# Three gathers ahead of a weighing, a shorter first run of side steps, and a norm tile on GpSimd

## The chip, the cores and the metric

The kernel runs on one core of a Trainium2 chip. A core has five engines with instruction queues of their own: TensorE (PE, matrix products and transposes into PSUM; its weight loads are listed as PEld), VectorE (DVE), ScalarE (ACT), GpSimd (POOL) and SyncE (SP, which here issues nearly all DMAs). Each engine takes its instructions strictly in the order in which the program wrote them, and waits for the others through semaphores. The metric is the device time of one execution in microseconds; lower is better.

## The reference

The model is four pairs of an attention and a feed-forward part on x of shape 8 x 512 x 128, all in float32, each part with a layer norm ahead of it and a residual addition behind it:

```python
x = x + _L0_attn_ref(_layernorm(x), ...)   # batch norm, sigmoids, attention without softmax
x = x + _L0_ffn_ref(_layernorm(x), ...)    # 16 experts on every 16-wide piece of a token, best 2
x = x + _L1_attn_ref(_layernorm(x), ...)   # linear attention
x = x + _L1_ffn_ref(_layernorm(x), ...)    # shared expert, and one of 8 for chosen tokens
x = x + _L2_attn_ref(_layernorm(x), ...)   # 16 heads, softmax over the queries
x = x + _L2_ffn_ref(_layernorm(x), ...)    # 8 low-rank experts, 2 given ones per token
x = x + _L3_attn_ref(_layernorm(x), ...)   # 21-tap convolution along the tokens
x = x + _L3_ffn_ref(_layernorm(x), ...)    # gated, weights and activations rounded to 4 bits
```

Two parts matter here. In layer 0's feed-forward every token is cut into 8 pieces of 16 numbers; a softmax over 16 experts is taken for each piece, the two best experts are kept with their weights, and their outputs are added:

```python
w = jax.nn.softmax(t @ expert_emb, axis=-1)
topw, topi = jax.lax.top_k(w, K)                       # K = 2 of 16
hmid = jax.nn.gelu(jnp.einsum('td,edi->tei', t, W1) + b1, approximate=False)
eo = jnp.einsum('tei,eio->teo', hmid, W2) + b2
comb = (jnp.take_along_axis(eo, topi[:, :, None], axis=1) * topw[:, :, None]).sum(axis=1)
```

In layer 2's feed-forward each token of the first 1024 has two given experts. Rows are ordered by expert, each expert is applied to its own rows, and the results go back to their tokens, weighted:

```python
order = jnp.argsort(flat_e, stable=True); bin_ids = flat_e[order]; tok = order // top_k
xr = x.reshape(T, hs)[tok]
for e in range(E):
    h = jax.nn.gelu(xr @ w1A[e].T @ w1B[e], approximate=False)
    out = out + (bin_ids == e)[:, None] * (h @ w2A[e].T @ w2B[e])
y = jnp.zeros((T, hs), xr.dtype).at[tok].add(flat_w[order][:, None] * out)
```

## The kernel before

x stays in SBUF as eight blocks (b = 0 to 7) of 512 tokens, each as four tiles (j) of 128 tokens by 128 features. The order of work on each engine is written out by hand: the program says in which order Python calls the pieces, and every engine's queue is the sequence of its instructions in that order.

**Layer 0, attention, second run.** After the batch norm, `run` walks a list of stages over the blocks; in iteration i each stage works on block i plus its lag, in the order of the list. For block b the residual is added (`attended`, L274), statistics are taken (`stats`: four bn_stats and bn_aggr on DVE, L732 and L734, then 1/sqrt on POOL, L246 and L247, and the scaled mean on POOL, L737). In the next iteration `scale` makes the four norm tiles `xn` (L743 on ACT, L349 on POOL). Its argument `own` says how many tiles ACT makes; the rest go to POOL. In the first run it is called with its default, three and one; in the second run with J = 4, all on ACT. `turned` transposes them on PE an iteration later, `hidden` and `logits` follow, `spikes` puts sigmoids on ACT and a product on POOL (L392), `biased` adds a bias on POOL (L352). The list also calls three steps of block 0's choice in each iteration once it is under way, and filler matmuls (`keep_clock`).

**Layer 0, experts.** There are 128 units (b, e), 16 experts for each block, worked through in pipeline order: at index n, the first product and the GELUs of unit n (`first_half`, L569 and L570 on ACT), then the second product of unit n - 2 on PE and its weighting on DVE (`second_half`, L582), then its addition on POOL (L588). The weights come from DRAM: `choice(b)` works out on DVE (and a little on POOL) which two experts each piece keeps, in twelve steps; the last transposes the result and writes it to the DRAM tensor `gates[b]` with four DMAs (L477). `spread` reads four experts' weights of a block, repeated over 16 partitions, into one of three buffers `gs` with eight DMAs (L550) on SP. `fetch` calls it for the k-th spread (block k // 4) once `gates` of that block has been written in program order and, from k = 3 on, not before 4 * (k - 2) units are done. The steps of the choices of blocks 1 to 7 and of some other preparations are side steps: `side` takes the next one. After the second half of each index one side step is taken, at indices 0 and 1 five each. Within an index, `fetch` comes before the side step.

**Layer 2, frames.** Layer 2's attention is 64 frames, one per pair of heads of a block. A frame n makes scores for two key tiles at a time (`scores(n, 0)` and `scores(n, 1)`: PE, the maximum on DVE, L1629, exponentials on ACT, L1635), scales the values by the sums (`weigh(n, 0)` and `weigh(n, 1)`: a reciprocal on DVE, L1649, a product on POOL, L1650), multiplies (`context(n)`, one frame later on PE), and projects queries, keys, values and output for the frames around it. Projections have two forms: `project(n)`, in half arrays in an interleaved order (L1556) with marks on SP (L1523) between, and the plain calls `queries`, `output`, `values` (L250). The plain form is taken in the frames listed in `moving`. Other work is hung into a frame at five hooks: P inside the first scores, V after them, G after the first weighing, D after the second scores, E after the second weighing. Steps are put there with `at(frame, hook, f)`.

**Expert rows.** Layer 2's feed-forward runs beside it for blocks 0 and 1, in class `Rows`. In frame 8b + 9 the eight sets of 128 normalised rows are scattered by POOL's indirect DMAs into ordered slots in DRAM; in frame 8b + 10 they are loaded, and `products` applies the experts to 15 slots, ending with `last(0)` and `last(1)`, which copy the results out of PSUM (L1894) and write them to `slots_out` (L1895). In frame 8b + 11, hook E, `back` gathers four of the eight sets of rows with indirect DMAs on POOL (L1933); in 8b + 12, hook G, the other four. `add` adds them to x on DVE, weighted (L1946), in frame 8b + 12, hook E, and 8b + 13, hook V.

Of the kernel before, what the change touches and what calls it, by code (L numbers as in the profile page):

```python
# [26 lines left out]
D = 128  # L27
NB = 8
TB = 512
J = TB // P  # L30
# [134 lines left out]
def body(ctx, tc, dram, spans, x_in, ib, it, ic, ei, out):  # L165
# [114 lines left out]
    def layer0():  # L280
# [7 lines left out]
        with ExitStack() as st:  # L288
# [54 lines left out]
            def scale(b, own=3):  # L343
                l0[b]["xn"] = xn = norm.tile([P, J, D], F32, tag="xn", name="xn")
                nb, rs = l0[b]["by"]
                scaled(xn, x[b], (nb, rs), own)
                for j in range(own, J):
                    r1, n1 = rs[:, j : j + 1], nb[:, j : j + 1]
                    nc.gpsimd.tensor_scalar(xn[:, j, :], x[b][:, j, :], r1, n1, ALU.mult, ALU.add)  # L349
# [139 lines left out]
            with (  # L489
                tc.tile_pool(name="a0h", bufs=1) as hp,  # L490
                tc.tile_pool(name="a0", bufs=2) as ap,
                psum({"one": 8}),
                tc.manual_schedule(),
            ):
                hs = [hp.tile([P, NB, TB], F32, tag=f"h{k}", name=f"h{k}") for k in range(3)]
                bst = [hp.tile([P, NB, 6], F32, tag=f"bst{k}", name=f"bst{k}") for k in range(3)]

                def run(stages, iterations):
                    for i in iterations:
                        for f, lag in stages:  # L500
                            if 0 <= i + lag < NB:
                                f(i + lag)

                run(
                    (
                        (scale, 2),
                        (stats, 3),
                        (turned, 1),
                        (project, 0),
                        (lambda b: biased(b, "bp"), -2),  # L510
                    ),
                    range(-3, NB + 2),
                )
                keep_clock(22)
                sc, bi = batch_norm()
                expand()
                run(
                    (
                        (turned, -2),
                        (lambda b: scale(b, J), -1),  # L520
                        (turn_v, 3),
                        (logits, -3),
                        (attended, 0),
                        (stats, 0),
                        (spikes, 4),
                        (gram, 2),
                        (gram_out, 1),
                        (hidden, -2),
                        (exponentials, -3),
                        (lambda b: chosen(3), -4),  # L530
                        (lambda b: biased(b, "bo"), -1),
                        (lambda b: keep_clock(6), -3 - NB // 2),
                    ),
                    range(-4, NB + 3),
                )
                chosen(20)
# [106 lines left out]
            with tc.manual_schedule():  # L643
# [36 lines left out]
                def second(n):  # L680

                    if n >= 2:
                        b, e = units[n - 2]
                        second_half(b, e, hms.pop(n - 2), gs[(n - 2) // 4][:, e % 4, :])
                        fetch(n - 1)
                    for _ in range(1 if n > 1 else 5):
                        side("V", n)

                for n in range(len(units) + 2):
# [716 lines left out]
    def late():  # L1406
# [11 lines left out]
        with tc.tile_pool(name="a2", bufs=2) as wp, tc.tile_pool(name="l3", bufs=1) as lp:  # L1418
# [5 lines left out]
            def at(frame, hook, *fs):  # L1424
                steps.setdefault((frame, hook), []).extend(fs)
# [273 lines left out]
            class Rows:  # L1699
# [116 lines left out]
                def products(self, meanwhile, ahead):  # L1816
# [63 lines left out]
                    def last(k, d):  # L1880
# [8 lines left out]
                                mm(two[g % 2][:, at_(i)], d[r, at_(i)], self.w2b(g))  # L1889
                        n = min(8, n_slots - 8 * k)  # L1890
                        dst = S[:, 8 * k : 8 * (k + 1), :].rearrange("p (i m) d -> p i m d", m=2)
                        for m, f in enumerate((nc.scalar.copy, nc.vector.tensor_copy)):
                            w_ = (n + 1 - m) // 2
                            f(dst[:, :w_, m, :], two[m][:, : w_ * P].rearrange("p (i d) -> p i d", d=D))  # L1894
                        nc.sync.dma_start(  # L1895
# [27 lines left out]
                    last(0, d0)  # L1923
                    last(1, d1)

                def back(self, js):
                    if js[0] == 0:
                        self.rows = both("cg").rearrange("p (n d) -> p n d", d=D)
                    for j in js:
                        for k in range(2):  # L1930
                            n = 2 * j + k
                            at_ = 8 * self.b + n
                            nc.gpsimd.indirect_dma_start(  # L1933
                                self.rows[:, n, :],
                                None,
                                slots_out[self.b],
                                bass.IndirectOffsetOnAxis(spots[:, at_ : at_ + 1], 0),
                            )

                def add(self, js):  # L1940
                    xb = x[self.b]
# [374 lines left out]
            for b in range(2):  # L2316
# [7 lines left out]
                at(8 * b + 9, "G", lambda r_=r_: r_.put((4,)))  # L2324
                at(8 * b + 9, "E", lambda r_=r_: r_.put((5, 6, 7)))
                at(8 * b + 10, "V", r_.load)
                at(8 * b + 11, "E", lambda r_=r_: r_.back((0, 1)))
                at(8 * b + 12, "G", lambda r_=r_: r_.back((2, 3)))
                at(8 * b + 12, "E", lambda r_=r_: r_.add((0, 1)))
                at(8 * b + 13, "V", lambda r_=r_: r_.add((2, 3)))  # L2330
            for b in range(NB - 1):
# [252 lines left out]
            with tc.manual_schedule():  # L2584
# [12 lines left out]
                            steps.pop((n, "S"), ()),  # L2597
                        )

                moving = {8 * b + k for b in range(2) for k in (9, 12)}  # L2600
                for n in range(N):
                    first_scores(n)
                    hook(n, "V")
# [74 lines left out]
```

## Time and profile before

| what | value |
|---|---|
| time, median of 3 runs | 1398.86 us (1398.42 to 1400.73) |
| profiled execution, its own time | 1393.95 us |
| its span, first to last instruction | 1392.2 us |
| PE busy | 1327.5 us, 95% |
| DVE busy | 1014.3 us, 73% |
| ACT busy | 1014.6 us, 73% |
| POOL busy | 642.4 us, 46% |
| DMA queue of SP and ACT | 28.3% of 16 engines' span |

The profile lists start times in microseconds from the first instruction. A line of a timeline names start, duration, engine, source line, operation, tile written and tiles read, and how often; in brackets stands the idle time before it and who ended it. The chain of waits is followed back from the last instruction: at each step to what released it or to the instruction before it on its engine, so what is on it is what set the end. SPq is SP's queue issuing a DMA; how long a DMA takes from there to landing is listed with the line that issues it. Matmuls are pipelined, so a busy PE is not one at its peak. In the frames, PE's granted clock is full; in one stretch of 3.4 us near 107 us it is half.

### The profile page before, as it was taken

The page shows a single profiled execution, that of the slowest core. Times are in us where ns is not written, and L with a number is a line of the kernel's source. Part 1 is how long each engine was busy: PE and PEld are TensorE (multiplying, and loading weights), DVE is VectorE, ACT ScalarE, POOL GpSimd, SP SyncE. Part 2 cuts the span into 40 slices and gives each one's busy share as a digit, 9 for nine tenths or more (in the row PEclk, how much of TensorE's full clock was granted, in tenths as well). Part 3 has the DMA queues.
Part 4 walks back from the last instruction along what each step waited for, and adds up shares of the span by engine and source line. Part 5 has one row for each costly group of instructions (what it writes and reads, how often), then busy time and mean ns, then how long its engine had stood idle before and what let it go on. Part 6 is the DMA issues. An engine that isn't in the chain of part 4 may idle for free.

```text
span 1392.2 us, 33106 instructions
## 1 busy us (share of the span) xinstructions
PE 1327.5 (95%) x12935; PEld 706.1 (51%) x12935; DVE 1014.3 (73%) x2148; ACT 1014.6 (73%) x2060; POOL 642.4 (46%) x748
## 2 busy tenths in 40 slices
PE   7889999999989999999999999999999999999997
PEld 3762222222267655547447545555555545555576
DVE  6785556666467778863783778888788797887876
ACT  7869999999978656665684686787767867667632
POOL 6645666666632533330472353353443634424432
PEclk9999999999999999999999999999999999999999
DMA  5019999999681010031211101101011010010000
GB/s 180 1 27 139 141 126 127 132 127 133 85 272 32 28 40 24 16 108 33 60 31 38 45 2 22 30 2 33 20 22 24 9 33 20 19 27 9 2 8 16
DMA packets 100713, 78.14 MB, mean 56 GB/s; under 512 B 52717, under 2 KB 93581, under 8 KB 96206
## 3 DMA queue, kind: packets, MB, share of 16 engines
q1 hardware_dynamic: 98828, 72.10, 28.3%
q0 software_dynamic: 1152, 2.36, 0.6%
q8 instruction: 102, 1.67, 0.6%
q10 hardware_dynamic: 578, 1.57, 0.3%
q14 instruction: 53, 0.43, 0.1%
HBM read 59.03 MB, written 16.97 MB: 55 GB/s over the span
## 4 chain that ended last, share of the span: by engine, by line
PE 52%; ACT 22%; DVE 19%; issue 3%; POOL 2%; DMA 1%; SPq 1%; DVEq 0%; ACTq 0%; POOLq 0%
PE ps L250 41%; PE ps L1556 8%; ACT hm L570 6%; ACT ex L1635 5%; DVE nm L1629 5%; ACT hm L569 3%; ACT prod L2023 2%; PE ps L2206 1%; DVE fa L1395 1%; DVE acc L2009 1%; DVE s L732 1%; ACT h L389 1%; DVE fa L1379 1%; DVE fsc L1374 1%; ACT q L1517 1%
## 5 line engine op out<-in xcount | busy, mean ns | idle before, releaser
L1635 ACT ACTIVATE ex<-ps,nm 128x512 f32<-128x512 f32 x512 | 345.2, 687 | 172.6 <-DVE nm L1629 170.2
L1629 DVE TENSOR_REDUCE nm<-ps 128x2 f32<-128x1024 f32 x256 | 301.1, 1211 | 41.9 <-PE ps L250 41.5
L250 PE MATMUL ps<-q,k 64*64 64x512 f32 (+1 forms) x2240 | 258.3, 565 | 7.4 <-ACT ex L1635 5.4
L250 PE MATMUL ps<-ex,vs 128*64 128x512 f32 x1024 | 233.9, 599 | 1.1 <-DVE sm L1649 1.1
L1650 POOL TENSOR_TENSOR vs<-v,sm 128x256 f32<-128x256 f32 x128 | 78.6, 614 | 296.6 <-DVE sm L1649 269.6
L588 POOL TENSOR_TENSOR acc<-acc,pr 128x512 f32<-128x512 f32 x119 | 165.6, 1391 | 93.8 <-DVE pr L582 85.8
L1556 PE MATMUL ps<-xt,blob_a 64*64 64x512 f32 x912 | 207.8, 589 | 0.5 <-SPq L1523 0.5
L570 ACT ACTIVATE hm<-ps,blob_f 128x1536 f32<-128x1536 f32 x128 | 196.2, 1533 | 0.0
L582 DVE SCALAR_TENSOR_TENSOR pr<-ps,blob_f,gs 128x512 f32<-128x512 f32 x120 | 90.1, 750 | 93.7 <-PE ps L250 72.1
L250 PEld LDWEIGHTS ps<-q,k 64*64 64x64 f32 x2240 | 74.6, 132 | 150.5 <-ACT ex L1635 77.6
L250 PE MATMUL ps<-h,w 32*128 32x512 f32 x1024 | 148.3, 643 | 1.1 <-ACT hm L569 0.6
L250 PEld LDWEIGHTS ps<-ex,vs 128*64 128x64 f32 x1024 | 68.1, 137 | 152.9 <-issue 126.7
L250 PE MATMUL ps<-hm,w 128*32 128x512 f32 x1024 | 136.9, 607 | 2.3 <-DVE pr L582 2.2
L2024 POOL TENSOR_TENSOR acs<-acs,prod 128x512 f32<-128x512 f32 x96 | 124.0, 1292 | 23.9 <-ACT prod L2023 19.4
L1556 PE MATMUL ps<-blob_a,ct 64*64 64x128 f32 x1824 | 118.6, 269 | 0.0
L1556 PE MATMUL ps<-blob_a,xt 64*64 64x128 f32 x1824 | 118.6, 269 | 0.0
L1556 PEld LDWEIGHTS ps<-blob_a,ct 64*64 64x64 f32 x1824 | 106.3, 133 | 0.0
L1635 ACT ACTIVATION_READ_ACCUMULATOR ex<-ps,nm 128x1 f32 x512 | 104.9, 205 | 0.0
L1556 PEld LDWEIGHTS ps<-blob_a,xt 64*64 64x64 f32 x1824 | 103.0, 133 | 0.0
L569 ACT ACTIVATE hm<-ps,blob_f 128x512 f32<-128x512 f32 x128 | 88.0, 687 | 13.3 <-PE ps L250 13.2
L250 PEld LDWEIGHTS ps<-h,w 32*128 32x128 f32 x1024 | 41.0, 184 | 109.1 <-ACT hm L569 100.5
L1556 PEld LDWEIGHTS ps<-xt,blob_a 64*64 64x64 f32 x912 | 61.7, 133 | 32.2 <-issue 28.7
(373 smaller groups left out, 2204.5 us busy)
## 6 DMA issues: line engine op xcount, KB each, us to landing
gs<-gates SPq DMA_DIRECT2D x248, 128.0 KB, 7.4
ht<-turned_h SPq DMA_DIRECT2D x20, 180.0 KB, 3.0
turned_h<-hb SPq DMA_DIRECT2D x40, 88.0 KB, 2.3
blob_f<-in_f SPq DMA_DIRECT2D x1, 2560.0 KB, 9.0
blob_a<-in_a SPq DMA_DIRECT2D x1, 2056.0 KB, 13.5
x<-in_x SPq DMA_DIRECT2D x8, 256.0 KB, 5.8
gates<-turned SPq DMA_DIRECT2D x32, 64.0 KB, 4.7
slots_in<-nought SPq DMA_DIRECT2D x8, 256.0 KB, 4.8
```

The lines of the kernel that those rows point to most:

```text
L250: nc.tensor.matmul(out_, lhs, rhs, start=start, stop=stop)
L389: nc.scalar.activation(hk, hk, AF.Sigmoid, bias=bi[:, k : k + 1], scale=sc[:, k : k + 1])
L569: nc.scalar.activation(hm[:, 0, :], p1, AF.Gelu, bias=bias)
L570: nc.scalar.activation(hm[:, 1:, :], p3, AF.Gelu, bias=bias)
L582: nc.vector.scalar_tensor_tensor(pr, po, f0["b2"][:, e : e + 1], gs, ALU.add, ALU.mult)
L588: nc.gpsimd.tensor_tensor(acc[:, b, :], acc[:, b, :], pr, ALU.add)
L1556: ins = nc.tensor.matmul(*args, **kw).ins
L1629: nc.vector.tensor_reduce(nm, ps, AX.X, ALU.max, negate=True)
L1635: nc.scalar.activation(ex[kt][:, i, :], ps[:, i, :], AF.Exp, bias=nm[:, i : i + 1], accum_out=sm[:, kt, i : i + 1],)
L1650: nc.gpsimd.tensor_tensor(vs[:, tiles, :, :], vs_[n][:, tiles, :].rearrange("p j (i n) -> p j i n", i=2), sm[:, tiles, :].unsqueeze(3).to_ ...
L2023: nc.scalar.activation(p, src, AF.Copy, scale=w)
L2024: nc.gpsimd.tensor_tensor(t["acs"], t["acs"], p, ALU.add)
```

## The change

Four edits. In layer 0's second run `scale` is called with its default: ACT makes three norm tiles and POOL the fourth, as in the first run. In the experts' loop the side steps at index 1 are three, not five; at index 0 they remain five. In `last` the first copy of slots 0 to 7, which ACT made, is made by DVE; the first copy of slots 8 to 14 stays on ACT. `back` takes the numbers of the eight gathers themselves, and the gathers are hung in differently: three in frame 8b + 11 at hook D, ahead of the second weighing, three at hook E behind it, and two in frame 8b + 12 at hook G, where there were four at E and four at G. Frames 11 and 19 join the frames with the plain form of projections.

```diff
                         (turned, -2),
-                        (lambda b: scale(b, J), -1),
+                        (scale, -1),
                         (turn_v, 3),
...
-                    for _ in range(1 if n > 1 else 5):
+                    for _ in range((5, 3)[n] if n < 2 else 1):
                         side("V", n)
...
-                        for m, f in enumerate((nc.scalar.copy, nc.vector.tensor_copy)):
+                        for m, f in enumerate(
+                            ((nc.vector.tensor_copy, nc.scalar.copy)[k], nc.vector.tensor_copy)
+                        ):
                             w_ = (n + 1 - m) // 2
...
-                def back(self, js):
-                    if js[0] == 0:
+                def back(self, ns):
+                    if ns[0] == 0:
                         self.rows = both("cg").rearrange("p (n d) -> p n d", d=D)
-                    for j in js:
-                        for k in range(2):
-                            n = 2 * j + k
-                            at_ = 8 * self.b + n
-                            nc.gpsimd.indirect_dma_start(
+                    for n in ns:
+                        at_ = 8 * self.b + n
+                        nc.gpsimd.indirect_dma_start(
...
-                at(8 * b + 11, "E", lambda r_=r_: r_.back((0, 1)))
-                at(8 * b + 12, "G", lambda r_=r_: r_.back((2, 3)))
+                at(8 * b + 11, "D", lambda r_=r_: r_.back((0, 1, 2)))
+                at(8 * b + 11, "E", lambda r_=r_: r_.back((3, 4, 5)))
+                at(8 * b + 12, "G", lambda r_=r_: r_.back((6, 7)))
...
-                moving = {8 * b + k for b in range(2) for k in (9, 12)}
+                moving = {8 * b + k for b in range(2) for k in (9, 11, 12)}
```

More of the change, by code (lines that the diff above doesn't have):

```diff
@@ L1924, in products @@
                     last(1, d1)
-                def back(self, js):
-                    if js[0] == 0:
+                def back(self, ns):
+                    if ns[0] == 0:
                         self.rows = both("cg").rearrange("p (n d) -> p n d", d=D)
-                    for j in js:
-                        for k in range(2):
-                            n = 2 * j + k
-                            at_ = 8 * self.b + n
[L1933 to L1938, printed above, removed]
+                    for n in ns:
+                        at_ = 8 * self.b + n
+                        nc.gpsimd.indirect_dma_start(
+                            self.rows[:, n, :],
+                            None,
+                            slots_out[self.b],
+                            bass.IndirectOffsetOnAxis(spots[:, at_ : at_ + 1], 0),
+                        )
                 def add(self, js):
```

## The prediction

> **What bounds the kernel now.** First the page's chain that ended last: PE holds 52%, ACT 22%, DVE 19%, POOL 2%, so a step counts only where it stands on that chain. All four edits lie in three stretches, so next I read the chain of waits in each, then the timelines of DVE, POOL and SP for what stands beside it.
>
> Layer 0's second run, chain of waits (start, us, what):
>
> ```profile
> 54.40 1.65 ACT xn L743 x4
> 56.04 2.12 ACT h L389 x3
> 58.16 0.04 ACT xt L361
> 58.20 0.33 issue
> 58.53 1.65 ACT xn L743 x4
> ...
> 62.30 0.58 ACT h L427
> ```
>
> ACT carries it until 62.9, and two groups of four norm tiles are on it; from 68.9 to 91.1 the chain is DVE's, and no ACT or POOL work is on it.
>
> The start of the experts, timelines of SP and DVE:
>
> ```profile
> 117.83 3.76 SPq L477 DMA_DIRECT2D gates<-turned  x4
> 122.08 9.08 SPq L550 DMA_DIRECT2D gs<-gates  x12
> ```
>
> ```profile
> 132.80 0.75 DVE L582 SCALAR_TENSOR_TENSOR pr<-ps,blob_f,gs 128x512 f32<-128x512 f32 x1 [0.72 <-PE ps L250]
> ...
> 135.25 0.75 DVE L582 SCALAR_TENSOR_TENSOR pr<-ps,blob_f,gs 128x512 f32<-128x512 f32 x1 [1.10 <-DMA gs<-gates]
> ...
> 143.39 0.75 DVE L582 SCALAR_TENSOR_TENSOR acc<-ps,blob_f,gs 128x512 f32<-128x512 f32 x1 [0.27 <-DMA gs<-gates]
> ```
>
> One unit lasts 2.07 us. Unit 12 comes 2.45 us after unit 11: 0.38 late, for the fourth spread (gs 3), whose eight transfers stand on SP behind the four writes of block 1's gates. ACT's next idle there is 0.27 and later not made up, so about 0.3 is lost. The DMA engines are full: 1.05 busy from 120 to 144 us.
>
> The end of the first expert rows and the frames after, chain of waits:
>
> ```profile
> 655.62 0.97 ACT ge L1894 x2
> 656.59 0.02 issue
> 656.61 0.57 DVE ge L1894
> 657.18 0.04 issue
> 657.22 1.09 PE ps L250 x8
> 658.31 3.45 PE ps L1556 x64
> 661.76 10.90 PE ps L250 x68
> ```
>
> Two ACT copies, then a DVE copy that waits for them, then PE without a gap to 672.7. POOL and DVE beside it:
>
> ```profile
> 662.91 0.61 POOL L1650 TENSOR_TENSOR vs<-v,sm 128x256 f32<-128x256 f32 x1 [4.87 <-DVE sm L1649]
> 663.70 1.02 POOL L1933 DMA_INDIRECT cg<-slots_out,spots  x1 [0.18 <-PE ps L250]
> ...
> 668.51 0.62 POOL L1650 TENSOR_TENSOR vs<-v,sm 128x256 f32<-128x256 f32 x1
> ...
> 673.08 0.94 POOL L1933 DMA_INDIRECT cg<-slots_out,spots  x1 [0.30 <-issue]
> ```
>
> ```profile
> 673.45 2.02 DVE L1946 SCALAR_TENSOR_TENSOR x<-cg,share,x 128x128 f32<-128x128 f32 x4
> 675.39 2.35 DVE L1629 TENSOR_REDUCE nm<-ps 128x2 f32<-128x1024 f32 x2
> 677.65 1.38 DVE L1946 SCALAR_TENSOR_TENSOR x<-cg,share,x 128x128 f32<-128x128 f32 x4
> ```
>
> The eight gathers are off the chain; only the additions feel them.
>
> **1. Norm tile on POOL: -0.8 us.** Eight ACT tiles leave, at 1.65/4 = 0.41 each; eight POOL instructions come, at 0.45 (L349's row from the first run). Only the tiles on the chain count: those of blocks 0 and 1, 2 x 0.41 = 0.82. From block 2 on POOL is as full as ACT: without a gap from 58.24 to 62.33, and block 1's tile goes ahead of block 2's rstd there. That rstd chain then ends at 62.8; ACT would have wanted it at 62.4, still 0.4 ahead of 63.23, and its group is 0.41 shorter, so the 0.8 stays. In DVE's stretch the gain is carried, not enlarged. At its end the last group starts at 93.08, but POOL is adding a bias from 93.00 to 94.27, so block 7's tile ends at 94.72, as ACT's fourth does now (94.73): nothing there, but ACT's next step starts 0.4 sooner and PE's, bound by the transposes ending at 95.11, 0.25 sooner. What is late behind the POOL tile: block 5's comes after two long POOL steps, 84.1 to 84.5, and its transpose on PE (81.64 now) is held by 2; PE has filler matmuls at 87.06 and 91.36 that take this up. Ends: -1.05 with the 0.25; +0.1 if two two-input DVE steps of the choice meet a tile and lose 0.45 each.
>
> Row against rule: DVE's comparison of L452 takes 0.68 alone and 1.46 beside POOL's bias at 73.82. The Trainium skill, "SBUF — State Buffer", section "Who interferes with whom", has it that a DVE instruction with two SBUF inputs and a GpSimd one that reads SBUF exclude each other for the whole instruction. By the rule at its worst, each of eight tiles would block such a step for its 0.45, and this part would be +2.8 rather than -0.8. By the rows, with each tile put behind its bias addition (75.1, 84.1, 89.0, 94.3), DVE is then in statistics, additions from PSUM, or at 75.1 in L452, which already waits for POOL. I take the rows.
>
> **2. First choice 5 and 3: +0.7 us.** No instruction comes or goes; twelve steps of block 1's choice end at unit index 5, not 3, and what follows is two indices later, with room: the side work ended at index 119 of 130, now 121. DVE has 2.07 - 0.75 - 0.69 = 0.6 spare in a unit. On SP the four gate writes now stand behind gs 3, because its fetch comes first at index 5. gs 2's last transfer is issued at 116.75 and takes 7.9 to land: 124.6. gs 3 needs its buffer (unit 3's product ends 116.7), goes out from 117.8, and lands one transfer a microsecond (issue and landing now: 122.08 + 5.8 to 128.01 + 6.8 = 127.9 to 134.8, seven steps): 132.6 instead of 134.8. Unit 12's 0.34 is gained. What is late next: the gate writes land behind it. Now they end 2.5 after gs 2 (121.02 + 6.1 = 127.1); the second and third land at 118.81 + 6.5 = 125.3 and 120.01 + 5.6 = 125.6, so without the last one's delay it would be 1.4; so 134.0 to 135.1. gs 4 reads those gates and may go out only then (now 128.53). Eight transfers from an empty queue: 2.2 to the first landing (the line's minimum), then 0.9 to 1.0 for each of seven (gs 4 now: 134.8 to 141.9): 142.5 to 144.3. DVE's five semaphore waits add 0.5 (134.8 to 135.25): 143.0 to 144.8 for unit 16, now at 143.39. I take the last write as late as it is now and gs 4's own rate: 135.1 + 2.2 + 7 x 0.9 + 0.5 = 144.1, +0.7. PE has one output bank and ACT one unit ahead, so a late product is lost time. Ends: -0.35 (no wait at either unit); +3.5 (144.8, plus one 2.12 us SP issue as at 122.08).
>
> **3. Copies of the expert rows: -0.9 us.** Two ACT copies (1.08 together) become one; the chain's DVE copy can start 0.5 sooner. PE's scores before it end at 655.67 + 1.09 = 656.76, so 657.22 can move by 0.46 at most. Twice (772.67 shows the same): -0.9. The added DVE copy (0.69 from 654.7) lies in DVE's idle 1.86 us before 656.61. If the DVE copy waits for something else: 0.
>
> **4. Gathers, and frames 11 and 19 unpaired: +0.6 us.**
> Projections in halves take 3.45 (658.31 to 661.76); in frame 12 the plain order takes 3.70 (668.96 to 672.66): +0.25 twice, +0.5; it drops two SP marks a frame, whose wait totals 0.5 in the page (low end 0).
> POOL: three gathers now stand ahead of the weighing at 662.91, and wait for the slot writes, whose landings were 3.3 to 5.0 after issue. Block 0: the second lands at 657.2 + 3.7, and 0.6 sooner by part 3, 660.3; three gathers take 3.55 (663.70 to 667.24); weighing until 664.5. PE's context starts at 663.2 and wants this half 1.83 later, 665.0: no wait. Block 1's write took 5.0: 777.2, plus 3.55 and 0.61 is 781.4 against 780.5: 0.9. As other rows land in 3.7, I take half, +0.5. Ends 0 and 1.8. The next three delay the half weighed at 668.51, wanted at 674.46: 5 us of cover. The last two end near 672, not 674.02.
> DVE's additions in frames 12 and 20 take 2.02 and 1.95, against 1.38 with POOL quiet. Without gathers beside them the weighing still is: -0.2 each, -0.4; ends -1.2 and 0.
>
> **Sum:** -0.8 + 0.7 - 0.9 + 0.5 + 0.5 - 0.4 = -0.4 us. It is made against the profiled execution, 1393.95 us (span 1392.2, 1.75 around it); the median of the runs is 4.9 above that, more than any term, so I carry the difference to the median: 1398.5.
>
> **Rivals.** (a) Slower: gs 4 comes late by its upper end, +3.5 in place of +0.7, total +2.4: 1401.3. It needs late gate writes and one long SP issue; for it the 1.41 and 2.12 us issues of gs 3, against it that most take 0.42. It turns the sign from unit 16's product later than 144.5. (b) All that the change is for and nothing lost: -1.05 - 0.35 - 0.9 + 0.5 - 1.2 = -3.0: 1395.9. For it gs 4's rate of 0.9; against it the write of 127.1. (c) The gathers hold the weighing in both frames, 1.8 for 0.5: +0.9, 1399.8. For it the 5.0 us landing, against it the 3.7. (d) The moves don't do what they say, as every one is hidden: 1398.9.
>
> **How the numbers follow.** 0.2% is 2.8 us, about what a measurement of this kernel can tell from no change. Forecast (with d) 0.50, nearly all within it; (b) 0.22, with 0.15 beyond; (a) 0.16, with 0.10 beyond once the runs' spread of 2.3 is added; (c) 0.12, with 0.04 beyond. Faster 0.18, same 0.66, slower 0.16. The range goes from (b) less 1.1 to (a) plus 0.9, half that spread each way: 1394.8 to 1402.2.
>
> **What would show it.** Right: ACT's groups L743 of three in the second run, POOL's eight L349 more; unit 12 on time, and DVE waiting for gs at unit 16; L1894 on ACT once per block, 0.45 off the PE gap; frame 12's additions under 1.9. Wrong: no wait at unit 16; a PE wait for vs in frame 12; DVE steps of the choice grown to over 1 us.

## The result, and the profile after

The changed kernel is slower by 0.2%: 1400.4 us median of 22 runs against 1397.04 us of the kernel before, run beside it, ratio 1.0021 (95% interval 1.0014 to 1.0029). The forecast difference was -0.4 us, within no change, so it missed by 3 to 4 us. The profiled execution of the changed kernel took 1398.32 us (span 1396.6); that of before 1393.95 (1392.2).

The chain that ended last, by engine and by line, from the page of the changed kernel:

```profile
PE 52%; DVE 18%; ACT 13%; DMA 10%; issue 3%; POOL 3%; SPq 1%; DVEq 0%; ACTq 0%; POOLq 0%
PE ps L250 42%; DMA gs<-gates 8%; PE ps L1556 7%; ACT ex L1635 5%; DVE nm L1629 5%; ACT prod L2023 2%; PE ps L2206 1%; DVE fa L1395 1%; DMA gates<-turned 1%; DVE acc L2009 1%; ACT h L389 1%; DVE fa L1379 1%; DVE fsc L1374 1%; ACT q L1517 1%; SPq L550 1%
```

Before, DMA held 1% of it. Now it holds 10%, nearly all of it the spreads of the experts' weights (`gs`), and ACT has lost as much (22% to 13%): in the experts, transfers set the pace where ACT did.

How far the changed profile lies behind that of before, found from the starts of the same instructions in both (counted from each one's first instruction):

| stretch, us of before | lag at its end | what happened in it |
|---|---|---|
| 0 to 51 | +0.69 | PE's clock was full from 16.4 us, before from 15.0 |
| 51 to 66 | -0.07 | norm tile on POOL: 0.76 gained |
| 66 to 104 | -0.52 | |
| 104 to 130 | +0.96 | two stretches of 3.4 us at half clock (105 to 112), before one |
| 130 to 143 | +0.34 | unit 12's late spread is gone: 0.62 gained |
| 143 to 378 | +1.53 | waits for `gs` at units 16, 24, 32, 48, 64, 96 |
| 378 to 655 | +1.57 | layer 1, frames 0 to 10 |
| 655 to 680 | +1.50 | frames 11 and 12: the edits' own gains and costs, 0.07 gained |
| 680 to 715 | +1.49 | |
| 715 to 771 | +4.90 | frame 18 |
| 771 to 800 | +4.68 | frames 19 and 20: 0.22 gained |
| 800 to 1320 | +4.38 | |

Layer 0's second run, timelines of ACT, PE and POOL:

```profile
55.08 1.26 ACT L743 ACTIVATE xn<-x,nb,rs 128x128 f32<-128x128 f32 x3 [1.75 <-POOL nb L737]
...
58.85 1.26 ACT L743 ACTIVATE xn<-x,nb,rs 128x128 f32<-128x128 f32 x3
```

```profile
81.47 0.56 PE L359 MATMUL ps<-blob_c,xn 128*128 128x128 f32 x3
84.44 0.33 PE L359 MATMUL ps<-blob_c,xn 128*128 128x128 f32 x1 [2.42 <-POOL xn L349]
84.61 1.83 PE L250 MATMUL ps<-emb,h 128*128 128x128 f32 x8
86.23 1.91 PE L250 MATMUL ps<-m,h 128*128 128x128 f32 x8
```

```profile
81.46 1.26 POOL L459 TENSOR_TENSOR eq<-eq,blob_ce 128x512 f32<-128x512 f32 x1 [1.11 <-DVE eq L458]
82.68 1.27 POOL L352 TENSOR_TENSOR x<-x,blob_bc 128x512 f32<-128x512 f32 x1
83.94 0.45 POOL L349 TENSOR_SCALAR xn<-x,rs,nb 128x128 f32<-128x128 f32 x1
```

The groups of three take 1.26, not 1.65. Block 5's tile comes behind two long POOL steps at 84.4, as forecast, and PE stands still for 2.42 us. What the forecast didn't have is the line after it: eight 128x128 products take 1.83 and 1.91 us. In the kernel before, the first eight took 1.16:

```profile
82.79 1.16 PE L250 MATMUL ps<-emb,h 128*128 128x128 f32 x8 [0.24 <-ACT h L427]
```

PE's clock was halved. Busy time by stretch, with the granted clock (the column of 1.00 and 0.50):

```profile
81.30:84.70 3.40, 0.98 (x6) 0.54 (x5) 3.19 (x14) 1.66 (x3) 3.07 (x4) 1.00 0.00 0
84.70:88.10 3.40, 3.40 (x18) 3.40 (x17) 3.33 (x7) 1.85 (x4) 3.24 (x5) 0.50 0.00 0
...
740.10:743.50 3.40, 1.33 (x30) 1.33 (x34) 1.27 (x2) 1.26 (x4) 0.52 (x1) 1.00 0.25 72
743.50:746.90 3.40, 3.40 (x27) 3.07 (x20) 1.32 (x3) 0.69 (x1) 0.61 (x1) 0.50 0.80 220
```

Twice the pattern is the same: a stretch in which PE was busy for 1.0 or 1.3 of 3.4 us, and behind it one at half clock.

The experts, timelines of SP and of DVE:

```profile
114.38 10.55 SPq L550 DMA_DIRECT2D gs<-gates  x11
125.66 4.24 SPq L477 DMA_DIRECT2D gates<-turned  x4
133.80 15.55 SPq L550 DMA_DIRECT2D gs<-gates  x20
```

```profile
144.48 0.75 DVE L582 SCALAR_TENSOR_TENSOR acc<-ps,blob_f,gs 128x512 f32<-128x512 f32 x1 [1.02 <-DMA gs<-gates]
...
179.88 0.75 DVE L582 SCALAR_TENSOR_TENSOR acc<-ps,blob_f,gs 128x512 f32<-128x512 f32 x1 [1.63 <-DMA gs<-gates]
...
214.86 0.75 DVE L582 SCALAR_TENSOR_TENSOR acc<-ps,blob_f,gs 128x512 f32<-128x512 f32 x1 [1.23 <-DMA gs<-gates]
...
249.64 0.75 DVE L582 SCALAR_TENSOR_TENSOR acc<-ps,blob_f,gs 128x512 f32<-128x512 f32 x1 [1.01 <-DMA gs<-gates]
```

The four gate writes of block 1 now stand behind gs 3 on SP, and gs 4 goes out at 133.8, where it was 128.53. Unit 16's product is at 144.48 (forecast: 144.1). But the first units of three later blocks wait too (the rows at 180, 215 and 250), where before the longest wait for a spread at any of these was 0.27.

Frames 11, 12 and 18, chain of waits:

```profile
657.19 0.50 ACT ge L1896
657.69 0.02 issue
657.71 0.04 DVE ge L1896
...
658.30 3.74 DMA slots_out<-ge
...
662.83 1.02 POOL cg L1933
663.86 0.30 issue
664.16 0.96 POOL cg L1933
665.12 0.30 issue
665.43 0.94 POOL cg L1933
666.37 0.02 issue
666.39 0.63 POOL vs L1650
667.03 0.04 issue
667.07 15.05 PE ps L250 x92
...
736.44 4.08 DMA slots_in<-xn,spots
```

One copy is left on ACT. The gathers do hold the weighing, so that PE waits for it, 0.21 us. The last line is the one that costs: in frame 18 the last scatter of block 1's rows takes 4.08 us to land. The kernel before, the same place:

```profile
734.96 2.22 DMA slots_in<-xn,spots
```

SP's load of those rows (L1741) waits for that landing, and the marks that let PE go on in the projections in halves (L1523) stand on SP behind the load. PE, the changed kernel:

```profile
742.17 0.65 PE L1556 MATMUL ps<-xt,blob_a 64*64 64x512 f32 x2 [2.31 <-SPq L1523]
```

Before, PE waited 0.48 us there. The longer pause, 1.83 us, and the half-clock stretch behind it, 1.58 us, are the 3.4 us of frame 18 in the table.

### The profile page after: what moved, and what is told of

The parts are those of the page before. It is cut to its first block, busy times and chain, and to the rows that moved or that the text cites. A ratio compares the mean times of both kernels' runs of the same rounds, so it can differ in the third digit from the quotient of the medians.

```text
span 1396.6 us, 32873 instructions
## 1 busy us (share of the span) xinstructions
PE 1332.9 (95%) x12815; PEld 707.1 (51%) x12815; DVE 1013.8 (73%) x2150; ACT 1010.8 (72%) x2050; POOL 646.5 (46%) x756
## 3 DMA queue, kind: packets, MB, share of 16 engines
q8 instruction: 101, 1.65, 0.5%
q10 hardware_dynamic: 578, 1.57, 0.3%
## 4 chain that ended last, share of the span: by engine, by line
PE 52%; DVE 18%; ACT 13%; DMA 10%; issue 3%; POOL 3%; SPq 1%; DVEq 0%; ACTq 0%; POOLq 0%
PE ps L250 42%; DMA gs<-gates 8%; PE ps L1556 7%; ACT ex L1635 5%; DVE nm L1629 5%; ACT prod L2023 2%; PE ps L2206 1%; DVE fa L1395 1%; DMA gates<-turned 1%; DVE acc L2009 1%; ACT h L389 1%; DVE fa L1379 1%; DVE fsc L1374 1%; ACT q L1517 1%; SPq L550 1%
## 5 line engine op out<-in xcount | busy, mean ns | idle before, releaser
L588 POOL TENSOR_TENSOR acc<-acc,pr 128x512 f32<-128x512 f32 x119 | 166.1, 1396 | 95.3 <-DVE pr L582 87.4
L1556 PE MATMUL ps<-xt,blob_a 64*64 64x512 f32 x880 | 201.1, 590 | 2.3 <-SPq L1523 2.3
L582 DVE SCALAR_TENSOR_TENSOR pr<-ps,blob_f,gs 128x512 f32<-128x512 f32 x120 | 90.0, 750 | 92.2 <-PE ps L250 75.7
L1556 PE MATMUL ps<-blob_a,xt 64*64 64x128 f32 x1760 | 114.9, 270 | 0.0
L1556 PE MATMUL ps<-blob_a,ct 64*64 64x128 f32 x1760 | 114.4, 269 | 0.0
L1556 PEld LDWEIGHTS ps<-blob_a,ct 64*64 64x64 f32 x1760 | 102.5, 133 | 0.0
L1556 PEld LDWEIGHTS ps<-blob_a,xt 64*64 64x64 f32 x1760 | 99.8, 133 | 0.0
```

Source lines behind the costliest of these rows:

```text
L582: nc.vector.scalar_tensor_tensor(pr, po, f0["b2"][:, e : e + 1], gs, ALU.add, ALU.mult)
L588: nc.gpsimd.tensor_tensor(acc[:, b, :], acc[:, b, :], pr, ALU.add)
L1556: ins = nc.tensor.matmul(*args, **kw).ins
```

## The experiments

Kernels that ran together are compared with the same runs of the kernel before; its median moved between such groups from 1396.1 to 1399.5 us, so small differences across groups say little. How little, one kernel shows that ran in two groups as e12 and e15: 0.9986 in one, 0.9965 in the other. The intervals cover the scatter of runs within a group, not that.

### Each part alone (e1 to e4)

The edits are the four hunks of the change, one at a time. Theories: the clock (the norm tile's pause halves it), the side steps, the gathers.

e1, the norm tile:

```diff
-                        (lambda b: scale(b, J), -1),
+                        (scale, -1),
```

> The kernel before with the norm tile of the second run on POOL, alone. Theory 1 (the loss is in TensorE's clock: PE waits for block 5's tile about 2.4 us near 82 us, and a half-clock window of 3.4 us follows): the ACT chain still gains 0.8 by 77 us, but a half window stands near 85 us, often a second one at 105 to 112 us, and the time is 0 to 2 us above before (ratio 1.000 to 1.0015). Theory 2 (the loss is in the side steps and the fourth spread): this edit alone gains its 0.8, ratio 0.9994, with no half window that before doesn't have. Theory 3 (the loss is in the gathers): as theory 2.

e2, the side steps:

```diff
-                    for _ in range(1 if n > 1 else 5):
+                    for _ in range((5, 3)[n] if n < 2 else 1):
```

> The kernel before with five and three first side steps, alone. Theory 1 (clock): +0.5 to +0.8 us from the fourth spread at unit 16 and nothing beside it, ratio 1.0005. Theory 2 (the side steps carry the loss): unit 16 late by 0.7, and a second step of about 1.2 us at unit 38 (190 us), so +1.5 to +2, ratio 1.0013, at an unchanged clock. Theory 3 (gathers): as theory 1.

e3, the copies:

```diff
-                        for m, f in enumerate((nc.scalar.copy, nc.vector.tensor_copy)):
+                        for m, f in enumerate(
+                            ((nc.vector.tensor_copy, nc.scalar.copy)[k], nc.vector.tensor_copy)
+                        ):
```

> The kernel before with the first copy of slots 0 to 7 on DVE, alone. All theories: PE's gap at 657 and at 773 us shorter by 0.46 each, -0.9 us, ratio 0.9993; if the copy waits for something else there, 1.0000.

e4, `back`, its three hooks and frames 11 and 19:

```diff
-                at(8 * b + 11, "E", lambda r_=r_: r_.back((0, 1)))
-                at(8 * b + 12, "G", lambda r_=r_: r_.back((2, 3)))
+                at(8 * b + 11, "D", lambda r_=r_: r_.back((0, 1, 2)))
+                at(8 * b + 11, "E", lambda r_=r_: r_.back((3, 4, 5)))
+                at(8 * b + 12, "G", lambda r_=r_: r_.back((6, 7)))
...
-                moving = {8 * b + k for b in range(2) for k in (9, 12)}
+                moving = {8 * b + k for b in range(2) for k in (9, 11, 12)}
```

> The kernel before with the gathers three, three and two and frames 11 and 19 in the plain form, alone. Theory 1 (clock) and theory 2 (side steps): between 0 and +1 us, ratio 1.000 to 1.0007, PE waiting for the weighed values once per block. Theory 3 (the gathers carry the loss: PE waits for the weighed values in both blocks, and the load of the ordered rows, the gathers' own transfers and the clock near 740 us add to it): +2.5 us or more, ratio 1.0018, with a half-clock window near 744 us.

Measured, against 1397.18 us:

| | median us | ratio, 95% interval | mean granted clock of the runs |
|---|---|---|---|
| e1 norm tile | 1396.45 | 0.9993 (0.9985 to 1.0002) | 0.9975 |
| e2 side steps | 1400.05 | 1.0023 (1.0014 to 1.0033) | 0.9965 |
| e3 copies | 1396.89 | 0.9997 (0.9988 to 1.0006) | 0.9986 |
| e4 gathers | 1397.43 | 0.9999 (0.9988 to 1.0009) | 0.9978 |
| before | 1397.18 | | 0.9977 |

The side steps alone lose as much as the whole change. In e2's profile unit 16 is later than in that of the changed kernel:

```profile
145.74 0.75 DVE L582 SCALAR_TENSOR_TENSOR acc<-ps,blob_f,gs 128x512 f32<-128x512 f32 x1 [3.27 <-DMA gs<-gates]
```

and a stretch at half clock follows it:

```profile
144.70:148.10 3.40, 1.56 (x16) 0.47 (x16) 1.77 (x3) 1.24 (x1) 0.00 (x0) 1.00 0.97 125
148.10:151.50 3.40, 3.40 (x20) 1.98 (x16) 1.16 (x3) 2.12 (x2) 1.65 (x1) 0.50 1.12 145
```

The second step that was expected at unit 38 doesn't show in e2; what comes on top stands here, 1.1 us more by unit 18. The first theory is out as the main cause: e1 does have the half-clock stretch behind block 5's tile (84.0 to 87.4), and is not slower.

### Is it the order on SP, or the later steps? (e5 to e8)

Two things come with five and three: the gate writes move behind gs 3 on SP, and DVE's steps of block 1's choice come two indices later.

e5:

```diff
-                    for _ in range(1 if n > 1 else 5):
+                    for _ in range((5, 4)[n] if n < 2 else 1):
```

> The kernel before with five and four first side steps: block 1's choice ends at index 4, so its gate writes still stand on SP ahead of the fourth spread (gs 3, index 5). Theory 2a (the loss comes from the order on SP: with five and three the fifth spread, gs 4, can go out only after writes that stand behind gs 3, so the transfers pause after gs 3 and the lead is gone for all later blocks): like before, ratio 0.9995 to 1.0005, gs 4 on time at unit 16, no wait of more than 0.3 at units 32, 48 and 64. Theory 2b (the loss comes from fewer side steps in the first indices, so that all that follows is late): about half of the loss of five and three, ratio 1.001.

e6, DVE's steps where they were, the writes behind gs 3:

```diff
                 nc.vector.transpose(g, left.rearrange("p g e -> p (g e)"))
+                if b == 1:
+                    yield "V"
+                    yield "V"
                 to = gates[b].rearrange("(c r) (j a s) -> a r j c s", c=4, j=J, a=4)
```

> The kernel before with five and five steps, but with the gate writes of block 1 held back by two side steps, so that they stand behind gs 3 on SP as in the changed kernel, while DVE's steps of that choice stay where they were. Theory 2a (order on SP): the loss of five and three comes back, ratio 1.0015 to 1.0025, DVE waits 1 to 3 us for gs at unit 16 and again at units 32 to 96. Theory 2b (DVE's steps late): ratio 1.000 to 1.0005, as DVE's work is as early as before.

e7, DVE's steps later, the writes ahead of gs 3:

```diff
-                        fetch(n - 1)
-                    for _ in range(1 if n > 1 else 5):
+                        if n != 5:
+                            fetch(n - 1)
+                    for _ in range((5, 3)[n] if n < 2 else 1):
                         side("V", n)
+                    if n == 5:
+                        fetch(n - 1)
```

> The kernel before with five and three, and at index 5 alone the side step is called ahead of the fetch, so that the gate writes stand ahead of gs 3 on SP again, while DVE's steps are as late as with five and three. Theory 2a (order on SP): the loss is gone, ratio 0.9995 to 1.0008, at most 1 us at unit 12 as gs 3 goes out about 0.5 us later than before. Theory 2b (DVE's steps late): the loss stays, ratio 1.002.

e8, the changed kernel without the side steps' edit:

```diff
-                    for _ in range((5, 3)[n] if n < 2 else 1):
+                    for _ in range(1 if n > 1 else 5):
```

> The changed kernel with five and five first side steps again. Theory 2 (the side steps alone carry the loss, and the other three parts add up as they did alone: 0.9993, 0.9997 and 0.9999): ratio 0.9990 against the kernel before, some 1.5 us less. If the parts disturb each other (through TensorE's clock or the vs wait): ratio 1.000 or more.

Measured, against 1396.23 us: e5 0.9992 (0.9982 to 1.0002), e6 1.0035 (1.0023 to 1.0048), e7 1.0008 (0.9996 to 1.0019), e8 1.0017 (1.0007 to 1.0027). It is the order on SP. e6 has DVE's work as early as before and loses most; e7 has it as late as in the change, and stays near before. The waits at units 32 to 96 that were expected of e6 didn't come. SP and unit 16 in e6 (its L585 is L582 elsewhere, its L480 and L553 are L477 and L550):

```profile
113.97 11.30 SPq L553 DMA_DIRECT2D gs<-gates  x12
125.96 4.59 SPq L480 DMA_DIRECT2D gates<-turned  x4
134.28 15.38 SPq L553 DMA_DIRECT2D gs<-gates  x20
```

```profile
145.82 0.75 DVE L585 SCALAR_TENSOR_TENSOR acc<-ps,blob_f,gs 128x512 f32<-128x512 f32 x1 [3.56 <-DMA gs<-gates]
```

SP in e7:

```profile
117.38 3.67 SPq L477 DMA_DIRECT2D gates<-turned  x4
121.47 26.79 SPq L550 DMA_DIRECT2D gs<-gates  x32
```

A measure that leaves out what happened earlier is the time from the first gate write of block 0 (93.45 in before, 93.31 in the changed kernel) to unit 16's product, and to the last unit's:

| order on SP | profiles | to unit 16 | to the last unit |
|---|---|---|---|
| writes ahead of gs 3 | before, e1, e3 to e5, e7 to e10, e12 to e15 | 49.05 to 50.73 | 288.8 to 291.1 |
| writes behind gs 3 | after, e2, e6, e11 | 51.17, 52.34, 51.73, 52.49 | 292.0, 293.6, 293.6, 293.9 |

The two ranges don't touch. With the writes behind gs 3 the transfers stop: gs 4 may go out only when writes that are queued behind gs 3's transfers have landed (gs 4 from 133.80 in the changed kernel, 134.28 in e6, 128.00 in e7). And little of the lead that is lost is won back, since a spread takes about as long as the four units that use it: eight transfers at 0.9 to 1.2 us, and four units at 2.07 are 8.3.

What follows unit 16 differs. In the changed kernel it is 1.23 us later than in before by this measure, and with the waits at the later spreads the last unit is 1.68 later. In e2, e6 and e11 the wait at unit 16 is longer (3.27, 3.56 and 4.49 us), one or two half-clock stretches stand behind it (148.1 to 151.5, 145.9 to 152.7 and 143.5 to 150.4), and the lag grows by 1.1, 2.4 and 1.9 us up to unit 18.

e8 answers the other half. The three parts that were harmless alone lose 0.17% together. Its mean clock is 0.9944, as low as the changed kernel's 0.9943, and its profile has the same late landing in frame 18 (4.00 us), PE waiting 2.24 us, and half clock behind it. e4 has it too (3.48 and 1.53), with no half clock.

So the losses seem to overlap rather than add: beside these three parts the side steps add only 0.04% (1.0021 against 1.0017, though in two groups), where alone they cost 0.23%. The traces fit this. Counted from the first gate write, e8 and the changed kernel are 0.79 and 0.48 us behind before at unit 15, after two half-clock stretches near 105 us, while e2, e6 and e11 are 0.61, 1.51 and 1.67 ahead. Engines that are late already wait less for gs 4.

### Frame 18 (e9 to e12)

The landing was 2.2 us in before, e1 to e3 and e5 to e7, and 3.48, 4.00 and 4.08 in e4, e8 and the changed kernel: those with the gathers part. The trace's transfers show a load of code, 16 KB on queue 8, that starts at 738.28 in the changed kernel, between the issue of that scatter (736.44) and its landing. In before the nearest such loads start at 731.21 and 742.62. The plain form of projections makes PE's program 120 matmuls shorter (12935 to 12815 on the page). Queue 8, which the page calls `instruction`, moved 102 packets in every kernel with 12935 matmuls, 101 with 12815, and 100 in e11 to e13 and e15 with 12695. So it brings PE's program, and a shorter program moves its loads.

e9:

```diff
-                moving = {8 * b + k for b in range(2) for k in (9, 12)}
+                moving = {8 * b + k for b in range(2) for k in (9, 11, 12)}
```

> The kernel before with frames 11 and 19 in the plain form of projections, gathers as before (four and four). In the three kernels with the whole gathers part the last scatter of block 1's rows lands 3.5 to 4.1 us after its issue, and PE pauses 1.5 to 2.3 us in frame 18 (740 us) behind the load that waits for it; in the seven others it lands in 2.2 and the pause is under 0.8. Theory 3a (PE's program is 120 matmuls shorter by the plain form, so that a 16 KB load of code falls on the last scatter): that late landing is here too, 3.5 us or more, a code load between 738 and 741 us, a pause of 1.5 or more. Theory 3b (the order of the gathers on POOL does it): landing 2.2, pause under 0.8. In time, 1.000 to 1.001 by either.

e10 is e4's edit without that line.

> The kernel before with the gathers three, three and two, and frames 11 and 19 left as they were (marks on SP, projections in halves). Theory 3a (code load): the last scatter of block 1 lands in 2.2 us and PE's pause in frame 18 is under 0.8. Theory 3b (order of the gathers): landing 3.5 or more, pause 1.5 or more. In frames 12 and 20, PE's wait for the weighed values 0 to 1.8 us per block by either; in time 0.999 to 1.001.

e11 and e12, from the changed kernel; e12 takes both hunks, e11 the first alone:

```diff
-                moving = {8 * b + k for b in range(2) for k in (9, 11, 12)}
+                moving = {8 * b + k for b in range(2) for k in (9, 10, 11, 12)}
...
-                    for _ in range((5, 3)[n] if n < 2 else 1):
+                    for _ in range((5, 4)[n] if n < 2 else 1):
```

> The changed kernel with frames 10 and 18 in the plain form too, so that no mark of PE's stands on SP behind the load that waits for the scatters. Theory 2 and 3a together: PE's pause near 740 us (2.3 in the changed kernel) and the half-clock window behind it are gone, some 2 to 3 us where they fell, so ratio 1.000 to 1.001 against the kernel before, where the changed kernel had 1.0021; the waits for gs stay. If the pause in frame 18 is not what costs there: ratio 1.002.

> The changed kernel with frames 10 and 18 in the plain form and the first side steps five and four instead of five and three. Theory 2a and 3a: both losses gone and the gains of the other parts kept, ratio 0.998 to 0.9995. If the losses lie elsewhere: 1.001 or more.

e9, chain of waits and PE's timeline:

```profile
736.17 3.71 DMA slots_in<-xn,spots
```

```profile
741.34 0.65 PE L1556 MATMUL ps<-xt,blob_a 64*64 64x512 f32 x2 [1.75 <-SPq L1523]
```

e10, the same:

```profile
734.83 2.22 DMA slots_in<-xn,spots
```

```profile
738.72 0.65 PE L1556 MATMUL ps<-xt,blob_a 64*64 64x512 f32 x2 [0.46 <-SPq L1523]
```

The plain form brings the late landing (its code load starts at 737.73), the gathers' order does not (742.56). So the form of projections in frames 11 and 19 costs in frame 18, where nothing was edited.

The traces also tie the landing to the code load. Of the scatters in frames 9 and 17 (`slots_in`, blocks 0 and 1) whose landing they show, fourteen have such a load starting 0.6 to 1.9 us behind their issue. Each of them lands 0.96 to 1.10 us behind the end of that load, which is 2.63 to 4.08 us after its issue; the 140 others take 2.21 to 2.46. What holds the scatter until the load is done isn't shown. Whether the half clock comes on top also counts: in e4 and e9, where it doesn't, the lag grows by 1.1 and 1.3 us between 715 and 748 us, in e8 and the changed kernel by 3.4.

e10's own price is elsewhere, in frame 20, PE's timeline:

```profile
782.63 1.94 PE L250 MATMUL ps<-ex,vs 128*64 128x512 f32 x8 [1.95 <-POOL vs L1650]
```

Here the weighing behind three gathers is late by 1.95 us; in the changed kernel, with the plain form in that frame, PE doesn't wait there.

In time, against 1396.13 us: e9 1.0019 (1.0006 to 1.0031), e10 1.0021 (1.0012 to 1.0030), e11 1.0003 (0.9993 to 1.0013), e12 0.9986 (0.9976 to 0.9996). e9 and e10 are both above what was expected (at most 1.001), and both halves of the gathers part lose where e4, with both, did not; e4 ran in another group and on another chip, and no run here explains that. e11 has no pause of PE above 0.35 us in frame 18, and regains most of the loss; that it still has the late gs 4 is plain on DVE:

```profile
144.53 0.75 DVE L582 SCALAR_TENSOR_TENSOR acc<-ps,blob_f,gs 128x512 f32<-128x512 f32 x1 [4.49 <-DMA gs<-gates]
```

Its engines were 3.1 us ahead of before at unit 15, and the transfers took all of it. e12, which differs from e11 in one side step, gains 0.17% on it and is 0.14% below before.

### The norm tile and the clock (e13 to e15)

e13, from e12:

```diff
-                        (scale, -1),
+                        (lambda b: scale(b, J), -1),
```

> The mended kernel of e12 without the norm tile on POOL (four on ACT again). Theory 4a (the tile's 0.8 us are kept, whatever the clock): 0.8 us slower than e12 on the same chip, ratio to before about 0.9992. Theory 4b (the 2.4 us pause of PE for block 5's tile, and the half-clock windows it brings, cost more than the 0.8): mean granted clock 0.001 to 0.002 higher than e12's 0.9955, and a time equal to e12's or lower, ratio 0.998 or less.

e14, from e12, 14 filler matmuls on PE ahead of block 5's transposes:

```diff
                     (
+                        (lambda b: b == 7 and keep_clock(14), 0),
                         (turned, -2),
```

> The mended kernel of e12 with 14 filler matmuls on PE ahead of block 5's transposes, so that PE's pause for the tile on POOL shrinks from 2.4 us to under 1. Theory 4b: the half window near 84 us is gone, mean granted clock 0.001 higher or more, and the time 0 to 1.5 us below e12's. Theory 4a: the clock may rise, and the time stays within 0.5 us of e12's.

e15 is e12 again. Beside e12 the kernel before had a median of 1396.13 us, beside e15 1399.46, and no run explains that; e13 to e15 are compared with each other.

> The mended kernel of e12 again, on the chip of the two kernels it is compared with: ratio to before 0.9976 to 0.9996 as there, mean granted clock 0.9955. Theories 4a and 4b differ in how e13 and e14 stand to it.

Measured, against 1399.46 us:

| | median us | ratio, 95% interval | mean granted clock of the runs |
|---|---|---|---|
| e13, no norm tile | 1393.38 | 0.9965 (0.9953 to 0.9978) | 0.9971 |
| e14, fillers | 1395.47 | 0.9973 (0.9963 to 0.9984) | 0.9959 |
| e15, as e12 | 1393.34 | 0.9965 (0.9953 to 0.9977) | 0.9956 |

Without the tile the clock is higher and the time the same, which is what theory 4b said; but the interval of 1.7 us on either side holds 0.8 too, so it isn't settled by this pair. e14 goes against 4b: in its profile the pause and the half clock near 84 us are gone, and the clock of the runs is still low and the time not better. So that pause alone isn't what keeps the clock low; e14's profile has half-clock stretches near 106, 393, 502 and 806 us. How the tile lowers it otherwise stays open; in the profiles two half-clock stretches in a row near 105 us show in the changed kernel, e8, e14 and e15, all with the tile, but in e1, e11 and e12 one or none.

## Why the prediction was wrong

Two terms failed, the plain form of part 4 and the size of part 2.

**1. Norm tile, -0.8.** The chain part was right: 0.76 gained between 51 and 66 us, the groups of three at 1.26, block 5's tile at 84.4 and PE held by 2.4. No DVE step of the choice grew: L452 takes 1.43, where it took 1.46, and block 4's tile behind it 0.88 instead of 0.45. The cover named for the hold of block 5 ("PE has filler matmuls at 87.06 and 91.36 that take this up") kept the time, but the step left out the clock: in five of the six traces with this pause (the changed kernel, e1, e8, e12 and e15, not e11) the next 3.4 us run at half. Alone the part measured 0.9993, -0.7 us by the medians; in the mended kernel of e12 its gain can't be told from nothing (e13 against e15).

**2. First choice five and three, +0.7.** The order on SP was read rightly, the size wasn't. There was no wait at unit 12, gs 4 went out late behind the writes, and the product came at 144.48 for 144.1. That it hit is luck, as two errors cancel: the last write landed at 133.66, not 135.1, and gs 4's eight transfers, taken as 2.2 + 7 x 0.9 = 8.5 us from the first issue to the last landing, took 10.3 (11.2 in e2, e6 and e11). "What is late next" also stopped at unit 16. The transfers had been read as full (1.05 busy from 120 to 144 us), and from a full resource lateness is handed on: units 24, 32, 48 and 64 waited 0.97, 1.63, 1.23 and 1.01. In the changed kernel's own profile that is +1.19 from 143 to 378 us against 0.62 gained at unit 12. Alone the part measured +2.9 us (e2), not +0.7, with the half clock behind unit 16 in it, which the step didn't have. Rival (a), +2.4, named the late writes, the sign and nearly the total, and was given 0.16; the point from which it was to decide, unit 16 later than 144.5, is where the changed kernel's own profile lies. But its total is near by luck: the long SP issue that it needed isn't there (gs 4's longest takes 0.91), and frame 18, the largest loss of the profile, isn't in it.

**3. Copies, -0.9.** One ACT copy of 0.50 is left, and PE's wait before the scores falls to 0.18. In e3's profile frames 11 and 19 gain 0.47 each, as forecast. In time 0.9997, -0.3 by the medians; the interval holds -0.9 and 0. In frame 12 of that profile PE also waits 1.50 for DVE; e1, which doesn't touch these frames, has such a wait too (0.81), and no run explains it.

**4. Gathers and frames 11 and 19, +0.6.** The wait for the weighed values came in block 0 (0.21) and not in block 1; without the plain form (e10) it is 0.58 and 1.95, so the upper end of 1.8 was real, and the plain form hides it. The additions take 1.59 and 1.58, not 2.02 and 1.95: 0.4 each, where 0.2 was taken. They take 1.59 in e1 to e3 as well, where the gathers stand as before but the additions start behind the last of them. The plain form costs 0.35 a frame, where 0.25 was taken. In their own frames parts 3 and 4 thus gain 0.3 us together, as the sum had it (-0.9 + 0.5 + 0.5 - 0.4). The failed step is the plain form all the same: it was priced at +0.25 a frame and two marks less, and not for what a shorter program does elsewhere. Frame 18, which the change doesn't touch, lost 3.41 us in the profile, of which the longer pause is 2.31 - 0.48 = 1.83; the other 1.58 come with the half clock behind it. With that pause taken away (e11, in another group) the ratio is 1.0003.

**The sum.** The profiled time of before was carried to a median of 1398.9, and beside the changed kernel before's median was 1397.04; so the predicted 1398.5 stands 1.9 below the measured 1400.4, while the forecast difference of -0.4 is off by 3.8 from the measured +3.4 of the medians (+2.9 by the ratio). The profiles differ by 4.4 us, and 3.4 of these are frame 18. The sum held gains from engines in a stretch that transfers pace, and took no account of the clock. Of the three signs named as wrong, the wait for vs in frame 12 did come, but it cost 0.2; of the larger losses, the wait at unit 16 stood among the signs named as right, and frame 18 among none.

The traces show when the clock falls: of all stretches of its 3.4 us grid in the seventeen traces, but for the first and last 20 us, each in which PE stood still for 1.86 us or more was followed by one at 0.50. Most with less were not, up to 1.83, but some were, with 0.4 to 1.8 (near 103, 383 and 497 us), and near 105 and 145 us a second half-clock stretch followed the first. The Trainium skill, "TensorE: Matmul & The Clock Gate", section "What's actually happening", has the clock fall after at least one idle window of about 3.4 us, in a free-running grid. The grid agrees (every such stretch here is 3.41 us or a multiple, but for the last before the end); a whole idle window wasn't needed.

## What to carry to other kernels

Where transfers run without a gap, an engine's gain may be none (e11 lost 3.1 us of lead at one unit): follow the queue, not the engine, and ask of every issue that is moved what now stands ahead of it, and for how many rounds the lateness lasts. A step put later on an engine may be free, while its DMA put behind another on the same queue is not; e6 and e7 tell the two apart in one pair. A pause of PE of some 2 us costs more than itself, as the next 3.4 us may run at half clock, and an edit that only shortens a program can move a load of code onto a transfer that someone waits for. Parts that were measured alone needn't add up: here three parts that cost nothing clear of noise alone cost 0.17% together, and a fourth that cost 0.23% alone added little to them (e8).

## What the runs showed of the hardware

Loads of code show in the trace as 16 KB transfers on queue 8. Between 600 and 800 us they take 0.9 to 1.7 us each, and in before and the changed kernel they stand 8 to 24 us apart from 640 us on. In the four traces in which one starts between the issue and the landing of frame 18's last scatter (the changed kernel, e4, e8 and e9), that scatter lands after 3.48 to 4.08 us; in the thirteen others, where none does, after 2.22 or 2.23. A scatter behind whose issue such a load starts, by 0.6 us or more, lands about 1.0 us behind the load's end.

The half clock's price depends on what paces the stretch. In frame 18, where PE paces, one stretch costs 1.6 us (3.41 less the 1.83 by which the pause grew). At the start of the experts it shows little: with the writes ahead of gs 3, unit 16's product stands 49.05 to 50.44 us behind the first gate write in the five profiles with no half-clock stretch near 105 us (e1, e3 to e5, e9), 49.33 to 50.30 in the five with one and 50.25 to 50.73 in the three with two. With spreads near their limit, most of what PE loses there was waiting anyway.
